# A macaron Mamba block on one core: short first and last chunks, rows loaded ahead, z's products and the gate as finer streams

## The chip, the cores and the metric

The kernel runs on one NeuronCore of one Trainium2 chip. The metric is the device time of one execution in microseconds (us), median of the runs; lower is better. The core has TensorE (PE, with its weight loads listed apart as PEld), VectorE (DVE), ScalarE (ACT), GpSimd (POOL) and SyncE (SP, which here only issues transfers). Each engine works through its own instructions in program order and waits on semaphores for the others.

## The reference, cut to what matters

x is 1 x 4096 x 1024, all in float32. Three residual steps follow one another: half a feed-forward step, a Mamba step, half a feed-forward step.

```python
def ffn(x):                      # weights rounded to -1, 0, 1 times their mean magnitude
    scale = mean(abs(weight)); w_t = clip(round(weight / (scale + EPS)), -1, 1)
    return x @ (w_t * scale).T + bias

def mamba(x):                    # D = 1024 channels, 16 states, a recurrence over 4096 tokens
    u, z = split(x @ W_in.T)
    u = silu(conv_b + sum(conv_w[:, k] * shifted(u, k) for k in range(4)))
    dt_r, B, C = split(u @ W_xproj.T)
    dt = softplus(dt_r @ W_dt.T + b_dt)
    h_t = exp(dt_t * A) * h_(t-1) + dt_t * B_t * u_t        # A = -exp(A_log)
    y_t = sum over states of h_t * C_t
    return ((y + u * Dskip) * silu(z)) @ W_out.T

x = x + 0.5 * ffn(layernorm(x)); x = x + mamba(layernorm(x)); x = x + 0.5 * ffn(layernorm(x))
```

## The kernel before

The 4096 tokens are cut into 16 chunks of T = 256 tokens, each of TT = 2 token tiles of 128. The channels lie on the partitions in 8 blocks of 128, and the recurrence is done in two halves of 4 blocks. For every chunk the kernel does, in this order of data:

- **Front** (`front`): rows are loaded (L236), normalized over channels (`stats` L390, L392, L394, L402 to L404; `normed` L409), transposed by PE (L425), split into a high and a low part (L453, L455) and multiplied with the ternary weights that stay on the chip (L497; for chunk 0, where these weights are just being made by DVE at L316 and L318, in `as_weights_come`, L528). The residual is added at L476; the bias reaches x by an accumulating transfer that POOL issues (L469). A second normalization follows, its transposes are copied to xT (L600), and PE forms the u products from W_in blocks that are streamed from memory through five shared weight buffers (L361, L629). `conv` applies the four taps (L559, L562 on ACT, L574 on DVE) and SiLU (L581).
- **Steps**: still in `front` and `rest`, PE projects u to dt_r, B and C (L641); B and C go to memory (L654) and come back spread over all partitions, one transfer for each half and state (`fetch`, L883, five bc buffers). `delta` forms dt (L710, L722). Then `rest` multiplies z's weights (L368, L677, SiLU at L696).
- **Recurrence**, for each half and state n: ACT forms the decays exp(dt A) (L913) in PSUM, POOL forms dt B u (L934) and adds what enters from the previous chunk (L941), DVE scans 2 x 2 blocks (L966, 512 columns each) and multiplies with C (L978), and PE sums over states by transposing each product into the y accumulator (`summed`, L998, 8 transposes). The skip term u * Dskip is the first of these products (L899). When a half is complete, `gate` multiplies y by silu(z) (L1015, one instruction for both token tiles).
- **Back** (`back`): the gated half is transposed back (`turned`, L752, L742), multiplied with W_out (L374, L760), added to x (L731), and the third step runs as the first did; the rows are written out (L772). The last chunk has a variant of its own (`last`), in which the first half's W_out products run before the second half is complete.

What sets the order of the work is a planner that runs while the program is built (`Streams`). Every piece of work above is a generator, a stream, that asks for an engine with an estimated duration and an earliest time; `run` always takes the request that can start first, ties by rank (the constants DECAY to FFN_C and Z), with a look-ahead `HOLD` by which an engine is kept for a better rank that is due soon. Buffers are handed round by `Buffers.take` and `put` with estimated times. The result is a fixed order on each engine and on SP's queue; on the chip each instruction then waits for what it truly needs, with everything behind it on its engine. So an instruction that is planned too early holds up its whole engine, and a transfer that waits for a buffer holds up every transfer behind it on SP's queue.

PSUM is used in full: three banks for general use, three for decays, and one double bank for y (`ys`, L998 writes it; chunk 0's first step borrows it). A chunk's y buffer is free again when its gate has read it.

Of the kernel before, what the change touches and what calls it, by code (L numbers as in the profile page):

```python
# [38 lines left out]
P = 128  # L39
T = 256  # L40
# [13 lines left out]
ISSUE, ADDED = 950, 6000  # L54
SWITCH = 1300

DECAY, ENTER, SUM, PREPARE, RECUR, GATE = 5, 1, 1, 0, 2, 2
FFN_A, NORM, U_PART, CONV, DELTA, OUT, FFN_C = 0, 0, 3, 0, 0, 2, 3

HOLD = 0, 0, 500, 100  # L60
# [3 lines left out]
class Streams:  # L64
# [32 lines left out]
    def run(self):  # L97
        hold = dict(zip(("PE", "DVE", "ACT", "POOL"), HOLD))
        while self.streams:
            todo = sorted(((self.start(s[2]), s[1], i) for i, s in enumerate(self.streams)))  # L100
# [73 lines left out]
def macaron_mamba_kernel(  # L174
# [16 lines left out]
    NC = S // T  # L191
# [10 lines left out]

    order = Streams()
# [6 lines left out]
    ys = buffers(1, [P, TT, OH], "y", pool_=psum)  # L210
    xs = buffers(6, [P, D], "x")
# [5 lines left out]
    szs = buffers(3, [P, TT, OH], "sz")  # L217
    dts = buffers(2, [P, HB, T], "dt")
    tmps = buffers(2, [P, D], "tmp")
    ups = buffers(3, [P, KER - 1 + T], "up")  # L220
# [3 lines left out]
    products = buffers(3, [P, HB, T], "p")  # L224
# [10 lines left out]
    def load_x(c, t):  # L235
        nc.sync.dma_start(x_tiles[c, t], x_in[(c * TT + t) * P : (c * TT + t + 1) * P, :])  # L236

    for t in range(TT):
        x_tiles[0, t] = xs.free.pop(0)[1]
        load_x(0, t)  # L240
# [100 lines left out]
    def streamed(load, n, ahead, rank):  # L341

        queue = []

        def fill():
            for i in range(n):
                yield lambda: 0 if len(queue) < ahead else INF
                w = yield from weights.take()
                load(i, w)
                queue.append((order.now + 5000, w))  # L350

        order.spawn(fill(), rank)
        return queue
# [26 lines left out]
    def stats(c, at, tiles=range(TT)):  # L380
# [5 lines left out]
        xn = {}  # L386
        for t in tiles:
            xn[t] = yield from tmps.take()
# [50 lines left out]
    def ffn(c, which, rank, at, tiles=range(TT)):  # L439
# [3 lines left out]
        def split(t):  # L443
# [6 lines left out]
            def cut(g, pt, at_):  # L450
# [12 lines left out]
            yield from transposed(xn, begin, cut, rank)  # L463
# [8 lines left out]
        def residual(t, cols, pf, at_):  # L472
# [4 lines left out]
            if (*key, t) != ("a", 0, 1):  # L477
                banks.put(pf, end)
# [36 lines left out]
    def as_weights_come(key, parts, residual, rank):  # L515

        for t in range(TT):
            yield from when("parts", key, t)
        y = yield from ys.take()
        groups = {(1, h): y[:, h, :] for h in range(2)}  # L520
        for h in range(2):
            groups[0, h] = yield from banks.take()
# [14 lines left out]
        for t in range(TT):  # L537
            los.put(parts[t][0], end)
            his.put(parts[t][1], end)
        for h in range(2):  # L540
            end = yield from when("ffn", key, 1, h * OH)
        ys.put(y, end)

    u, sz, dt, xd, bc_dram, over = {}, {}, {}, {}, {}, {}


    def hand_over(c, blk, up, at):
        end = yield pool(140, at)
        nc.gpsimd.tensor_copy(halo[:, blk, :], up[:, T:])
        ready["halo", c, blk] = end  # L550

    def conv(c, blk, pp, at):
        half, b = divmod(blk, HB)
        up = yield from ups.take()
        ub, rows_ = u[c, half][:, b, :], pp[:, blk % 2, :]
# [3 lines left out]
        nc.scalar.copy(up[:, KER - 1 :], rows_)  # L559
# [11 lines left out]
        for k in range(KER - 1):  # L571
            end = yield dve(405, end + (REACH if k == 0 else 115), True)
# [6 lines left out]
        if len(done) == HB:  # L579
            end = yield act(D, end + REACH, "silu")  # L580
            nc.scalar.activation(flat(u[c, half]), flat(u[c, half]), AF.Silu)  # L581
            ready["u", c, half] = end + REACH

    def front():
        for c in range(NC):
            yield FFN_A
            at = [3500, 5000]
            for t in range(TT if c else 0):
                x_tiles[c, t] = yield from xs.take()
                load_x(c, t)  # L590
                at[t] = order.now + 5000
            ends = yield from ffn(c, "a", FFN_A, at)
            yield NORM
            queue = streamed(u_weights, NB, 2, U_PART)
            ln, rows_, at = yield from stats(c, ends)
# [12 lines left out]
            for t in range(TT):  # L608
# [3 lines left out]
            for t in range(TT):  # L612
# [5 lines left out]
            for pair in range(NB // 2):  # L618
                if 2 * pair % HB == 0:
                    u[c, 2 * pair // HB] = yield from us.take()  # L620
                pp = yield from banks.take()
                pp = pp.rearrange("p (j t) -> p j t", t=T)
                for j in range(2):
                    w = yield from arrived(queue)
                    wt = w.rearrange("p (k m) -> p k m", m=P)
                    for k in range(NB):
                        if k % 4 == 0:
                            end = yield pe(8 * T * FULL)
                        nc.tensor.matmul(  # L629
                            pp[:, j, :], wt[:, k, :], xT[:, k, :], start=(k == 0), stop=(k == NB - 1)  # L630
# [3 lines left out]
            yield DELTA  # L634
            px = yield from banks.take()
            for half in range(2):
                at = yield from when("u", c, half)
                end = yield pe(2 * HB * T * FULL)
                for b in range(HB):
                    k = half * HB + b  # L640
                    nc.tensor.matmul(  # L641
                        px[:NXD, :T], wx[:, k, :], u[c, half][:, b, :], start=(k == 0), stop=(k == NB - 1)
                    )
            xd[c] = yield from xds.take()
            end = yield act(T, end + REACH)
            nc.scalar.copy(xd[c][RANK:NXD, 1, :], px[RANK:NXD, :T])
            for j in range(2):
                end = yield act(T)
                nc.scalar.copy(xd[c][j * RANK : (j + 1) * RANK, 0, :], px[:RANK, :T])
            banks.put(px, end)  # L650
            bc_dram[c] = dram.tile([NST, 2, T], F32, tag="bc", name=f"bcd_{c}")
            for j in range(2):
                part_ = slice(RANK + j * NST, RANK + (j + 1) * NST)
                nc.sync.dma_start(bc_dram[c][:, j, :], xd[c][part_, 1, :])  # L654
            ready["bc", c] = end + 2500
            yield from delta(c, 0, end + REACH)
            order.spawn(rest(c, xT), DELTA)
# [441 lines left out]
```

## Time and profile before

| | |
|---|---|
| median of 3 runs | 2726.5 us (2725.86 to 2727.03) |
| the profiled execution | 2725.84 us, its span 2724.1 us |
| busy PE / DVE / ACT / POOL | 2568.1 / 2288.3 / 2001.4 / 1815.6 us |
| first recurrence scan (DVE L966) starts | 104.2 us |
| last scan starts, last gate starts | 2668.2 us, 2675.8 us |
| moved by DMA | 410.8 MB, mean 151 GB/s |

The span is the time from the first to the last instruction on the core. Busy time is the union of an engine's instructions; PE's instructions are pipelined, so that eight listed at 1.04 us together start every 0.109 us. An idle time is put down to the instruction that ended it. Columns of the stretches of time further on: stretch, its length, busy time of the five rows with the number of instructions, the granted TensorE clock (1.00 is full), the share of time for which the DMA engines moved data, and GB/s.

### The profile page before, as it was taken

Reading aid. Unit: us, or ns where it says so; the run is one execution under the profiler, and the core shown is the slowest. Engines: PE = TensorE matmul, PEld = TensorE weight load, DVE = VectorE, ACT = ScalarE, POOL = GpSimd, SP = SyncE. Lnnn points to the kernel's source line nnn. Section 1 sums busy time; section 2 is a strip of 40 time slices with the busy share of each in tenths; the row PEclk is TensorE's granted clock in tenths of the full one; section 3 lists DMA queues with packets and bytes.
Section 4 is the critical chain, followed back from the end, with each engine's and each line's share of the span. In section 5 each row is a group of like instructions: output and inputs, shape, how many; then the busy total and the mean of one; then the engine's idle time right before and its main releaser. Section 6 shows DMA issues by size and latency. Waiting matters only on the chain. (4 is left out here: it accounts for less than half of the span.)

```text
span 2724.1 us, 41050 instructions
## 1 busy us (share of the span) xinstructions
PE 2568.1 (94%) x14082; PEld 2199.6 (81%) x14082; DVE 2288.3 (84%) x2404; ACT 2001.4 (73%) x4202; POOL 1815.6 (67%) x1657
## 2 busy tenths in 40 slices
PE   5797989999999999999999999999999999999988
PEld 4686878888788787888878788887888878788866
DVE  4498898978899798888879799898889879788883
ACT  3678677787877778777787877778787777877662
POOL 0367767766677585767757577686767857577761
PEclk9897999999999999999999999999999999999999
DMA  4443536455454545546554454655545554554533
GB/s 158 146 130 103 168 106 216 132 166 149 134 173 140 179 151 153 155 129 184 166 162 144 140 167 132 182 162 155 153 140 167 159 172 146 150 157 133 182 85 109
DMA packets 218553, 410.82 MB, mean 151 GB/s; under 512 B 19172, under 2 KB 85860, under 8 KB 218344
## 3 DMA queue, kind: packets, MB, share of 16 engines
q1 hardware_dynamic: 209128, 374.65, 43.3%
q0 software_dynamic: 9216, 33.56, 6.8%
q8 instruction: 110, 1.80, 0.3%
q14 instruction: 99, 0.81, 0.1%
HBM read 390.82 MB, written 17.31 MB: 150 GB/s over the span
## 5 line engine op out<-in xcount | busy, mean ns | idle before, releaser
L934 POOL TENSOR_TENSOR h<-u,bc 128x1024 f32<-128x1024 f32 x512 | 1223.2, 2389 | 421.7 <-ACT da L913 171.1
L966 DVE TENSOR_TENSOR_SCAN h<-da,h 128x512 f32<-128x512 f32 x1024 | 1207.7, 1206 | 125.6 <-ACT da L913 99.7
L913 ACT ACTIVATE da<-dt,pr 128x255 f32<-128x255 f32 x2048 | 938.6, 473 | 61.9 <-DVE h L966 32.9
L978 DVE TENSOR_TENSOR p<-h,bc 128x1024 f32<-128x1024 f32 x512 | 658.7, 1286 | 6.6 <-PE y L998 6.4
L998 PE MATMUL y<-ident,p 128*128 128x128 f32 x4352 | 572.5, 278 | 79.5 <-DVE p L978 61.1
L998 PEld LDWEIGHTS y<-ident,p 128*128 128x128 f32 x4352 | 503.9, 143 | 151.5 <-DVE p L978 95.4
L629 PE MATMUL bank<-xT,weight 128*128 128x256 f32 x2048 | 474.7, 382 | 11.4 <-ACT u L562 8.6
L677 PE MATMUL bank<-weight,xT 128*128 128x256 f32 x2048 | 474.7, 380 | 9.2 <-DMA weight<-in_w_in 9.2
L760 PE MATMUL bank<-weight,u 128*128 128x256 f32 x2016 | 467.3, 381 | 2.2 <-DMA weight<-in_w_out 1.9
L629 PEld LDWEIGHTS bank<-xT,weight 128*128 128x128 f32 x2048 | 378.6, 190 | 69.9 <-ACT u L562 21.3
L677 PEld LDWEIGHTS bank<-weight,xT 128*128 128x128 f32 x2048 | 380.2, 191 | 56.7 <-ACT da L913 9.9
L760 PEld LDWEIGHTS bank<-weight,u 128*128 128x128 f32 x2016 | 370.9, 191 | 47.2 <-DMA weight<-in_w_out 2.1
L949 ACT COPY state<-h 128x4 f32<-128x4 f32 x512 | 99.2, 194 | 292.5 <-DVE h L966 287.5
L941 POOL TENSOR_TENSOR h<-h,over 128x4 f32<-128x4 f32 x512 | 262.5, 513 | 25.2
L497 PE MATMUL bank<-wf,lo 128*128 128x512 f32 x976 | 252.3, 400 | 3.7 <-DVE lo L455 2.4
L574 DVE SCALAR_TENSOR_TENSOR u<-up,pr,u 128x256 f32<-128x256 f32 x384 | 206.4, 570 | 55.2 <-ACT u L562 42.6
L497 PE MATMUL bank<-wf,hi 128*128 128x512 f32 x976 | 245.8, 394 | 0.0
L497 PEld LDWEIGHTS bank<-wf,lo 128*128 128x128 f32 x976 | 177.7, 188 | 48.4 <-issue 4.0
L497 PEld LDWEIGHTS bank<-wf,hi 128*128 128x128 f32 x976 | 181.7, 188 | 43.0 <-issue 4.3
L865 POOL TENSOR_TENSOR over<-pr,dt 128x64 f32<-128x64 f32 x32 | 24.9, 778 | 211.3 <-ACT dt L722 211.3
L476 DVE SCALAR_TENSOR_TENSOR x<-bank,hscl,x 128x512 f32<-128x512 f32 x124 | 91.2, 737 | 71.9 <-PE bank L497 71.8
L425 PE MATMUL bank<-ident,tmp 128*128 128x128 f32 x756 | 115.9, 285 | 27.1 <-ACT tmp L409 23.4
(98 smaller groups left out, 2125.0 us busy)
## 6 DMA issues: line engine op xcount, KB each, us to landing
bc<-bcd SPq DMA_DIRECT2D x512, 256.0 KB, 3.7
weight<-in_w_out SPq DMA_DIRECT2D x128, 512.0 KB, 5.1
weight<-in_w_in SPq DMA_DIRECT2D x128, 512.0 KB, 3.7
weight<-in_w_in SPq DMA_DIRECT2D x256, 256.0 KB, 4.2
x<-hbias POOLq DMA_DIRECT2D x64, 512.0 KB, 7.9
x<-in_x SPq DMA_DIRECT2D x32, 512.0 KB, 7.3
out<-x SPq DMA_DIRECT2D x30, 512.0 KB, 4.9
weight<-in_w_ffn SPq DMA_DIRECT2D x5, 512.0 KB, 7.4
```

The costliest lines, as they stand in the source:

```text
L425: nc.tensor.matmul(pt[:, j * P : (j + 1) * P], xn[:, k * P : (k + 1) * P], ident, start=(j == 0), stop=(j == 3), is_transpose=True, skip_g ...
L497: nc.tensor.matmul(pf, x[:, k, :], wf[:, k, cols], start=(x is lo and k == 0), stop=(x is hi and k == NB - 1),)
L574: nc.vector.scalar_tensor_tensor(ub, up[:, k : k + T], tap, ub, ALU.mult, ALU.add)
L629: nc.tensor.matmul(pp[:, j, :], wt[:, k, :], xT[:, k, :], start=(k == 0), stop=(k == NB - 1))
L677: nc.tensor.matmul(pp[:, t, :], xT[:, k, t * P : (t + 1) * P], wt[:, :, i, :], start=(k == 0 and t == 0), stop=(k == NB - 1), skip_group_c ...
L760: nc.tensor.matmul(po[:, t, :], yT[:, b, t * P : (t + 1) * P], wt[:, b, :], start=(half == 0 and t == 0 and b == 0), stop=(half == 1 and b ...
L913: nc.scalar.activation(da[:, i, 1:], dt[c, half][:, b, 1:], AF.Exp, scale=a_neg[:, half * HB + b, n : n + 1],)
L934: nc.gpsimd.tensor_tensor(h, u[c, half], bc[:, 0:1, :].to_broadcast([P, HB, T]), ALU.mult)
L941: nc.gpsimd.tensor_tensor(h[:, :, 0], h[:, :, 0], over[c, half][:, :, n], ALU.add)
L966: nc.vector.tensor_tensor_scan(rows_, flat(da), rows_, 0.0, ALU.mult, ALU.add)
L978: nc.vector.tensor_tensor(p, h, bc[:, 1:2, :].to_broadcast([P, HB, T]), ALU.mult)
L998: nc.tensor.matmul(y[:, t, b * P : (b + 1) * P], p[:, b, t * P : (t + 1) * P], ident, start=(n < 0 and b == 0), stop=(n == NST - 1 and b = ...
```

## The change

The sequence is cut into 17 chunks: 128 tokens, 15 times 256, 128 tokens. Work tiles keep their shapes, and `cut` gives a view of the part that a short chunk uses. Further:

- `rows_ahead` is a stream of its own that loads the rows of later chunks as soon as one of the x buffers (7 for 6) is free; a buffer counts as free as soon as its output transfer is issued, where before 6 us were added.
- z's products (`gates`) and the projection with dt (`steps`) are two streams that start together when the u products have been issued; before, z's followed the projection.
- y is two single-bank buffers, one for each token tile; each tile is gated by itself when its last state has been summed, and transposed back tile by tile. Chunk 0's first step needs no y bank any more.
- Buffers: products 4 for 3, ups 4 for 3, z's sz 2 for 3; W_in's u blocks are streamed 3 ahead for 2, W_out's 2 ahead for 3.
- The planner gets other ranks, look-aheads and margins (`LATE_P`, `LATE_E`, 6,500 ns for a weight block), and a penalty `TABLE` for a request that would change ACT's function table.

```diff
-ISSUE, ADDED = 950, 6000
+ISSUE, ADDED = 950, 12000
-DECAY, ENTER, SUM, PREPARE, RECUR, GATE = 5, 1, 1, 0, 2, 2
-FFN_A, NORM, U_PART, CONV, DELTA, OUT, FFN_C = 0, 0, 3, 0, 0, 2, 3
-HOLD = 0, 0, 500, 100
+LATE_P, LATE_E = 300, 700
+AHEAD = 3
+DECAY, ENTER, SUM, PREPARE, RECUR, GATE = 5, 4, 1, 0, 5, 1
+FFN_A, NORM, U_PART, CONV, DELTA, OUT, FFN_C = 0, 4, 3, 0, 0, 2, 3
+TABLE = 300
+HOLD = 250, 0, 0, 0
...
-    NC = S // T
+    sizes = [P] + [T] * ((S - 2 * P) // T) + [P]
+    starts = [sum(sizes[:c]) for c in range(len(sizes))]
+    NC = len(sizes)
...
+    def cut(tile_, c, n):
+        t = sizes[c]
+        return flat(tile_)[:, : n * t].rearrange("p (b t) -> p b t", t=t)
...
-    ys = buffers(1, [P, TT, OH], "y", pool_=psum)
-    xs = buffers(6, [P, D], "x")
+    ys = buffers(TT, [P, OH], "y", pool_=psum)
+    xs = buffers(7, [P, D], "x")
-    szs = buffers(3, [P, TT, OH], "sz")
+    szs = buffers(2, [P, TT, OH], "sz")
-    products = buffers(3, [P, HB, T], "p")
+    products = buffers(4, [P, HB, T], "p")
...
+    def rows_ahead():
+        for c in range(1, NC):
+            for t in tiles_of(c):
+                x_tiles[c, t] = yield from xs.take()
+                load_x(c, t)
+                ready["x", c, t] = order.now + 5000
...
-            queue = streamed(u_weights, NB, 2, U_PART)
+            queue = streamed(u_weights, NB, 3, U_PART)
...
+            order.spawn(gates(c, xT), Z[0])
+            order.spawn(steps(c), DELTA)
...
-                xs.put(x_tiles.pop((c, t)), order.now + 6000)
+                xs.put(x_tiles.pop((c, t)), order.now + 0)
...
-            end = yield pe(D * TURN)
-            for t in range(TT):
+            for t in tiles_of(c):
+                if first:
+                    y[t] = yield from ys.take()
+                end = yield pe(OH * TURN)
...
+                if n + 1 == NST:
+                    order.spawn(gate(c, half, t, y[t], end + REACH), GATE)
...
-    def gate(c, half, y, at):
+    def gate(c, half, t, y, at):
         yield from when("z", c, half)
-        z = sz[c, half]
-        end = yield dve(1170, at)
-        nc.vector.tensor_tensor(flat(z), flat(y), flat(z), ALU.mult)
+        z = sz[c, half][:, t, :]
+        end = yield dve(650, at)
+        nc.vector.tensor_tensor(z, y, z, ALU.mult)
         ys.put(y, end + REACH)
-        ready["gate", c, half] = end + REACH
+        ready["gate", c, half, t] = end + REACH
...
+        (AHEAD, rows_ahead()),
```

## The prediction, made before the changed kernel was run

> **What bounds the kernel now.** I read the page's busy times first, then stretches of time, then who waits for whom on PE, then the timeline at the two ends.
>
> ```profile
> PE 2568.1 (94%) x14082; PEld 2199.6 (81%) x14082; DVE 2288.3 (84%) x2404; ACT 2001.4 (73%) x4202; POOL 1815.6 (67%) x1657
> ```
>
> PE leads, but 94% is a mean over unlike stages. The stretches separate them (columns as described with the profile above):
>
> ```profile
> 37.00:54.00 17.00, 7.04 (x32) 6.00 (x31) 3.23 (x7) 8.53 (x13) 1.69 (x6) 0.76 0.00 1
> 96.00:112.00 16.00, 6.75 (x21) 4.59 (x22) 5.09 (x5) 11.61 (x24) 9.14 (x8) 0.50 0.65 215
> 112.00:209.00 97.00, 94.59 (x524) 82.17 (x523) 85.78 (x90) 75.17 (x160) 67.07 (x69) 0.99 0.47 139
> 209.00:248.00 39.00, 22.13 (x108) 18.33 (x107) 32.44 (x31) 32.14 (x65) 29.12 (x24) 0.65 0.33 91
> 500.00:1000.00 500.00, 486.23 (x2720) 418.64 (x2719) 433.87 (x454) 383.53 (x807) 344.63 (x316) 1.00 0.52 155
> 2612.00:2625.00 13.00, 6.97 (x46) 6.34 (x47) 6.03 (x6) 11.35 (x19) 7.64 (x9) 0.79 0.12 40
> 2646.00:2672.00 26.00, 16.31 (x73) 13.75 (x73) 24.66 (x23) 11.30 (x29) 15.37 (x10) 0.67 0.53 173
> ```
>
> In the long middle PE is 97.2% busy at full clock: it is the bound there, and DVE (87%) is not. At the start and the end there are holes, and in each the granted clock falls too (0.50 to 0.79), so what PE still does in them is stretched. In the middle the remaining idle time has few owners (microseconds, times, longest, from 500 to 2500 us):
>
> ```profile
> PE y L998 <- DVE p L978: 21.6, 31, 1.3
> PE y L998 <- DVE sz L1015: 14.5, 11, 1.3
> PE bank L752 <- DVE x L476: 9.3, 11, 0.8
> ```
>
> The gate waits at L1015 recur once per chunk: 11 stand between 819.1 and 2445.8 us, so a chunk takes 162.67 us, and 16 take 2602.7. The span is 2724.1, so 121.4 us are the price of filling and draining. The timeline of the hole at 230 us shows what it is:
>
> ```profile
> 230.25 1.97 PE L998 MATMUL y<-ident,p 128*128 128x128 f32 x8 [6.70 <-DVE p L978]
> 233.81 1.97 PE L998 MATMUL y<-ident,p 128*128 128x128 f32 x8 [1.60 <-DVE p L978]
> ```
>
> PE has nothing left but one sum per state, waits for DVE's product each time, and at the low clock takes 1.97 us for eight transposes that take 1.04 elsewhere. The page's chain of waits agrees for the other end: its last 55 us are PE lines L760 and L497.
>
> **The change, part by part.** *The yardstick.* Fifteen full chunks and two halves are again 16 chunk equivalents, so 2602.7 us stay as long as the middle's pace stays. To be priced are the fill, the drain, the pace, and what an extra chunk adds to PE. PE's rates at full clock, from the timeline: 0.229 us for a matmul of 512 columns (L497), 0.216 for 256 (L629: eight in 1.73), 0.109 for a transpose of 128 (L998: eight in 0.87).
>
> *An extra chunk on PE.* u and the projection stream half the columns per weight block in a short chunk; the other products count by token tile and don't change. A pass of 128 columns is not in the trace; from below it is half of 0.216, from above the 0.143 us of one weight load (L998's PEld). 320 such passes in the two short chunks: 0 to +11 us. I take 0, since transposes, which have the same shape, start every 0.109.
>
> *The fill.* "Lost" is the length less PE's work at full rate. Before: until the first step's last matmul at 40.9, 16 transposes and 64 matmuls are 16.4 us of work, lost 24.5; the second normalization to 50.8, lost 9.9; transposes and u to 88.5, lost 7.4; projection and dt to 112, lost 14.9; 112 to 209, 3.4; the hole to 248, 16.9 idle and 0.35 of 22.1 by the clock, 24.6. Sum 84.7.
>
> After, the order on the engines is known, the times are not. DVE makes the ternary weights until 37.2 as before, but with 32 matmuls in place of 64 PE ends 1.2 us later, at 38.4: work 8.2, lost 30.2, which is 5.7 *more* than before. One tile's residual (two L476, 1.5 us) and one tile's normalization (5.3 us, as the tail's single tile takes from L390 to L425) reach 45.2: lost 6.8. u is 128 passes of 0.109, or 13.9 us; the supply is slower, since three buffers turn over in landing 3.7 + use 1.75 + issue 0.6 = 6.0 us, 2.0 a block, 16 for eight, and I take 17: ends 63, lost 2.7. Projection, dt, the first bc and the first scan took 15.7 us and have fixed parts (table loads 1.28, the transfer out and in 1.5 + 3.7); I take 13.5, so the first scan moves from 104.2 to about 77. PE need not stand still there: with z's stream apart, the order has three z blocks (5.2 us) and chunk 1's transposes and first step (16.4 us) next, whose rows are there; lost 4. Then chunk 0's recurrence: per state two scans of 1.165/2 and a product of 1.2/2 us, each with about 0.065 of fixed cost on top, 1.96 us, times 32 is 63 us, with chunk 1's conv and splits on DVE about 80. PE's work for this time is 14.8 (sums) + 8.6 (z) + 14.7 + 1.75 + 27.7 + 1.7 = 69; before it was about 107 against 118 of recurrence alone with as much added. A hole of 12 stays. Sum 56, so **-29**; with the old hole whole -16, with none -41.
>
> *Rows ahead.* Six row loads (3 MB) now stand on SP's queue before hbias, W_out and W_in. Until 40 us, 9.7 MB moved before (300 and 184 GB/s in the two 20 us stretches), now 12.2; at 300 GB/s that is 41 us, so it fits under the ternary stage and the normalization with 4 us to spare. Nothing taken; if not hidden, up to +4 of the 13 above.
>
> *The drain.* Before, 2600 to 2724 loses 24.7 idle and 8.9 by clock, 33.6 in all: the hole at 2612, the lone sums at 2646 to 2672, and the last step. After, the last recurrence is 63 us instead of 113 and has chunk 15's W_out and third step (27.6 + 14.7) beside 14.8 of sums; in the order only six sums are left after the last of it, each about 1.9 us with 0.9 of work, so -7 there, and about -3 at the first hole. Against it, the single last tile has nothing beside its normalization, where before the first tile's ran under W_out: 7.2 us from L731 to L455 against 3.4 exposed, +4. **-6**, from -15 to +5.
>
> *The pace.* Gate by tile: a sum for tile 0 of the next half needs only tile 0's gate, issued while tile 1 is summed. That removes the 14.5 us row but for one wait in six, -12 in 2000 us; DVE pays 32 gates more at a fixed 0.127 (402 ns for 256 columns at L731, 677 for 512 at L455), 4 us, under its 13% of slack. The later planned readiness of products and the fourth product buffer act on the 21.6, the shorter bank cycles on the 9.3; nothing shows how far, from all of it to none. I take a quarter, -8. That is -20 per 2000 us, 1.6 per chunk, **-24** over 15; all waits gone is 4.1 a chunk, -62. In the other direction I allow +1 a chunk, +15: two sz buffers for three, and SP below. Table loads on ACT fall from 181 to 175; ACT is idle 27%, nothing.
>
> A rule of the Trainium skill speaks against the short chunks: "Perfetto Trace Analysis", section "Optimizing Scalar/DVE Operations", puts about 60 ns of fixed cost on each DVE instruction and advises larger ones. By it the 162 added DVE instructions would be 10 us; the rows' 0.13 us make 21. The sum is the same by both, as DVE's slack covers either, and only in the 80 us after the first scan does it lengthen DVE's path, which the 1.96 us holds already.
>
> *Sum.* 2724.1 - 29 - 6 - 24 + 0 = 2665, and 1.7 us around the span gives 2667; the median runs 0.7 above the profiled execution: **2668**.
>
> **The rivals.**
>
> 1. *Only the ends gain.* The margins merely move the waits on PE and the pace stays 162.7: 2726.5 - 35 = 2692. For it: the 31 waits on p are each under 1.3 us, jitter of a plan rather than a structure. Against: the gate wait is structural and comes once per chunk.
> 2. *All of it.* The waits in the middle nearly vanish and the start has no hole: -41 - 6 - 50, 2630. Against: PE's order still waits for some engine in every row.
> 3. *SP's queue (slower).* In the new order the load into an x buffer stands right behind the output from the same buffer, and behind it the other output, two W_out blocks and bc loads. Before, this wait (SP L236 for the output) was 2.3 us in six times; an output lands after 4.9. Fifteen times 4.9 is 74 us; if all reach PE and the pace gains nothing, 2726.5 - 35 + 74 = 2765. It decides from 2.3 us a chunk. Against: four bc transfers go out just before, a buffer's turn is 5 x 3.53 = 17.7 us, of which landing and use take about 12, so some 6 us are slack.
> 4. *The start doesn't move.* u starves on W_in, or the six row loads delay the weights, and the first scan stays past 95 us: about 2710 with some pace gained.
>
> **How the numbers follow.** Forecast 0.50 (its own range 2652 to 2684), rival 1 0.22, rival 2 0.10, rival 3 0.10, rival 4 0.08. About 0.2%, 5 us, is what this kernel's measurement can tell. Slower holds rival 3 (0.10), no change a third of rival 4 (0.03), faster the rest, 0.87. The range takes in the forecast, rival 1, rival 4 to its middle and the near half of rival 2: 2636 to 2708.
>
> **What would show it.** First scan near 77 us (rows above 95: rival 4). No stretch of 39 us at clock 0.65 after it. A chunk period of 161 us from gate to gate and the row PE y <- DVE gate under 3 us in 2000 (162.7: rival 1). SP's row-load wait for the output: expected about 5 us a chunk, with no PE wait for W_out or DVE wait for bc behind it; if these appear, rival 3. The prediction is wrong if the middle's PE share falls below 97%, or if the last tile's chain is longer than the sums it replaces.

## The result, and the profile after

The changed kernel takes **2698.03 us** (median of 4 runs, 2693.4 to 2698.7) against 2726.24 us for the kernel before, measured beside it: a ratio of 0.9893, 95% interval 0.988 to 0.9905. It is 28 us faster; 58 were forecast. The time lies outside the forecast's own range (2652 to 2684) and nearest to rival 1 (2692); only the wide range, which takes the rivals in, holds it. The profiled span is 2696.9 us.

Busy times of the changed kernel, as listed on its page:

```profile
PE 2567.8 (95%) x14242; PEld 2199.8 (82%) x14242; DVE 2320.2 (86%) x2564; ACT 2017.8 (75%) x4401; POOL 1773.4 (66%) x1747
```

PE is as busy as before (2568.1), to 0.3 us: the whole gain is idle time. Stretches of the changed kernel (columns as in the table before; the bounds are its own events: end of the first step, start and end of chunk 0's u, first scan, chunk 1's first scan, and the drain):

```profile
38.40:45.40 7.00, 1.83 (x9) 1.61 (x9) 0.00 (x0) 4.11 (x6) 1.31 (x5) 0.50 0.00 0
45.40:69.70 24.30, 19.95 (x134) 18.48 (x134) 7.24 (x21) 8.97 (x23) 2.15 (x14) 0.85 0.52 156
69.70:90.50 20.80, 17.06 (x83) 14.15 (x82) 4.51 (x10) 16.02 (x32) 6.18 (x13) 0.84 0.60 162
90.50:201.70 111.20, 100.50 (x520) 82.73 (x520) 84.59 (x133) 93.33 (x243) 64.25 (x97) 0.98 0.44 131
500.00:1000.00 500.00, 485.98 (x2711) 416.86 (x2710) 450.76 (x470) 379.55 (x816) 340.49 (x323) 1.00 0.53 156
1500.00:2000.00 500.00, 492.14 (x2750) 423.76 (x2749) 441.14 (x468) 385.02 (x816) 344.20 (x323) 1.00 0.52 157
2657.00:2674.50 17.50, 16.82 (x72) 13.95 (x72) 1.97 (x4) 0.59 (x1) 0.00 (x0) 0.90 0.56 181
2674.50:2696.90 22.40, 11.92 (x41) 9.15 (x40) 3.31 (x5) 4.80 (x7) 2.15 (x5) 0.77 0.19 47
```

The 39 us at clock 0.65 behind the first recurrence are gone (0.98 up to chunk 1's first scan). The middle has two parts: from 500 to 1000 us PE is no busier than before (486.23), and only later does it reach 98.4%. The end has a stretch of 22.4 us in which PE works for half the time. PE's waits from 500 to 2500 us, and SP's row for the loads of x (waited for: us, times, longest):

```profile
PE bank L653 <- ACT u L578: 10.2, 14, 1.7
PE bank L784 <- DVE x L496: 8.8, 11, 0.8
PE bank L445 <- ACT sz L721: 5.2, 11, 1.4
PE y L1045 <- DVE p L1022: 4.7, 11, 0.5
...
PE y L1045 <- DVE sz L1062: 0.3, 1, 0.3
...
SPq L256 <- DMA out<-x: 47.4, 22, 4.6
```

The waits on products fell from 21.6 to 4.7 us, those on the gate from 14.5 to 0.3; the waits for banks that ACT reads grew (10.2 and 5.2 us; before, u's had 2.4 and sz's no row). SP waits 47.4 us for outputs in front of row loads, and no wait of PE for W_out or of DVE for bc stands behind it.

**Where the time came from.** I use the prediction's measure, "lost" = time less PE's work so far at full rate. That work is 2472.2 us in all, at the prediction's rates and 0.136 us for each of dt's matmuls, so that the span is 2472.2 plus what is lost; matmuls that run slower than the prediction's rate count as lost too. The loss is cut by PE's work done, and the period is the distance of the chunks' first scans, a mean over six chunks in the steady part. The experiments are in the same table, so that it can be read beside them (medians as each run has them, the other columns from the profiled execution; us):

| kernel | lost to 200 of work | 200 to 1000 | 1000 to 2350 | from 2350 | period | median |
|---|---|---|---|---|---|---|
| before | 90.7 | 52.4 | 71.5 | 37.2 | 162.6 | 2726.2 |
| changed | 76.0 | 52.5 | 57.9 | 38.3 | 160.7 | 2698.0 |
| pad | 70.7 | 51.4 | 56.7 | 39.4 | 160.7 | 2695.3 |
| uniform | 103.5 | 44.7 | 54.2 | 27.4 | 160.7 | 2705.0 |
| defer | 107.1 | 50.1 | 57.2 | 39.6 | 160.7 | 2727.7 |
| first2 | 109.9 | 58.5 | 55.2 | 27.5 | 160.7 | 2722.3 |
| wholegate | 79.8 | 68.1 | 145.3 | 38.4 | 169.3 | 2805.2 |
| tilegate | 91.7 | 82.4 | 103.4 | 36.4 | 166.4 | 2792.5 |
| oldconst | 114.3 | 79.2 | 88.1 | 38.9 | 162.1 | 2794.6 |
| serialz | 96.8 | 67.6 | 96.6 | 37.0 | 164.8 | 2777.3 |
| norows | 80.9 | 81.6 | 96.6 | 47.9 | 168.3 | 2782.1 |
| upback | 74.9 | 51.8 | 56.7 | 38.1 | 160.6 | 2694.9 |
| drainfill | 74.4 | 53.1 | 57.8 | 34.5 | 160.7 | 2691.2 |
| both | 74.0 | 52.0 | 56.4 | 33.9 | 160.6 | 2690.4 |

Against the kernel before, the change gains 14.7 at the start, nothing from 200 to 1000 us of work, 13.6 in the rest of the middle, and loses 1.1 in the drain: 27.2, the difference of the spans. One caution on small differences: the changed kernel and pad have the same instructions in the same order, and their first columns differ by 5.3; the changed kernel's profiled execution is the slowest of its four (2698.7), pad's the fastest of its four (2692.2).

### The profile page after: what moved, and what is told of

Read it like the earlier page. It is cut to its first block, busy times and chain, and to the rows that moved or that the text cites. A ratio compares the mean times of both kernels' runs of the same rounds, so it can differ in the third digit from the quotient of the medians.

```text
span 2696.9 us, 41854 instructions
## 1 busy us (share of the span) xinstructions
PE 2567.8 (95%) x14242; PEld 2199.8 (82%) x14242; DVE 2320.2 (86%) x2564; ACT 2017.8 (75%) x4401; POOL 1773.4 (66%) x1747
## 4 chain that ended last, share of the span: by engine, by line
PE 33%; ACT 7%; DVE 7%; issue 4%; POOL 4%; DMA 0%; POOLq 0%; DVEq 0%; SPq 0%
PE bank L516 8%; PE bank L792 6%; PE bank L653 6%; PE y L1045 5%; PE bank L706 5%; DVE h L1009 3%; DVE p L1022 3%; POOL h L977 2%; ACT da L955 2%; PE bank L671 1%; PE bank L445 1%; ACT tmp L414 1%; ACT tmp L429 1%; ACT u L578 1%; ACT dt L754 1%
## 5 line engine op out<-in xcount | busy, mean ns | idle before, releaser
L977 POOL TENSOR_TENSOR h<-u,bc 128x1024 f32<-128x1024 f32 (+1 forms) x544 | 1230.5, 2262 | 419.1 <-ACT da L955 206.6
L1009 DVE TENSOR_TENSOR_SCAN h<-da,h 128x512 f32<-128x512 f32 (+1 forms) x1088 | 1216.7, 1143 | 132.4 <-ACT da L955 68.7
L955 ACT ACTIVATE da<-dt,pr 128x255 f32<-128x255 f32 (+1 forms) x2176 | 982.5, 462 | 381.9 <-DVE h L1009 341.2
L1022 DVE TENSOR_TENSOR p<-h,bc 128x1024 f32<-128x1024 f32 (+1 forms) x544 | 695.0, 1278 | 0.1
L1045 PEld LDWEIGHTS y<-ident,p 128*128 128x128 f32 x4352 | 505.7, 142 | 83.2 <-DVE p L1022 28.8
L653 PE MATMUL bank<-xT,weight 128*128 128x256 f32 (+1 forms) x2176 | 476.6, 372 | 20.9 <-ACT u L578 17.6
L706 PE MATMUL bank<-weight,xT 128*128 128x256 f32 x2048 | 487.1, 383 | 3.8 <-ACT sz L721 1.4
L516 PE MATMUL bank<-wf,lo 128*128 128x512 f32 x1008 | 268.9, 409 | 4.4 <-DVE x L496 2.5
L516 PE MATMUL bank<-wf,hi 128*128 128x512 f32 x1008 | 259.5, 399 | 0.0
L590 DVE SCALAR_TENSOR_TENSOR u<-up,pr,u 128x256 f32<-128x256 f32 (+1 forms) x408 | 197.5, 517 | 48.8 <-POOL up L573 22.8
L516 PEld LDWEIGHTS bank<-wf,lo 128*128 128x128 f32 x1008 | 185.6, 191 | 52.3 <-DVE x L496 6.4
L516 PEld LDWEIGHTS bank<-wf,hi 128*128 128x128 f32 x1008 | 187.4, 189 | 46.6 <-issue 3.3
L445 PE MATMUL bank<-ident,tmp 128*128 128x128 f32 x760 | 115.9, 281 | 33.9 <-ACT tmp L429 22.4
L445 PEld LDWEIGHTS bank<-ident,tmp 128*128 128x128 f32 x760 | 93.5, 144 | 53.8 <-ACT tmp L429 24.3
```

Source lines behind the costliest of these rows:

```text
L445: nc.tensor.matmul(pt[:, j * P : (j + 1) * P], xn[:, k * P : (k + 1) * P], ident, start=(j == 0), stop=(j == 3), is_transpose=True, skip_g ...
L516: nc.tensor.matmul(pf, x[:, k, :], wf[:, k, cols], start=(x is lo and k == 0), stop=(x is hi and k == NB - 1),)
L590: nc.vector.scalar_tensor_tensor(ub, up[:, k : k + T], tap, ub, ALU.mult, ALU.add)
L653: nc.tensor.matmul(pp[:, j, :T], wt[:, k, :], xT[:, k, :T], start=(k == 0), stop=(k == NB - 1))
L706: nc.tensor.matmul(pp[:, t, :], xT[:, k, t * P : (t + 1) * P], wt[:, :, i, :], start=(k == 0 and t == 0), stop=(k == NB - 1), skip_group_c ...
L955: nc.scalar.activation(da[:, i, 1:], dt[c, half][:, b, 1:], AF.Exp, scale=a_neg[:, half * HB + b, n : n + 1],)
```

## The experiments

Every kernel is the changed one with the edit shown, but for tilegate, which starts from the kernel before. The kernel before ran beside each (2725.3 to 2726.5 us); ratios are to it.

### The sizes: uniform, first2, defer

**uniform** has 16 equal chunks and all the rest of the change; the only further edits are that chunk 0's first step borrows the y banks, as before, and that the clearing of decay banks for a short last chunk falls away.

```diff
-    sizes = [P] + [T] * ((S - 2 * P) // T) + [P]
+    sizes = [T] * (S // T)
```

> The changed kernel with 16 equal chunks of 256 tokens, all else kept (chunk 0's first step borrows the two y banks for its second tile). By PE's work done (0.229, 0.216 and 0.109 us an instruction) the changed kernel had lost 15 us less than the one before after 200 us of work, and nothing less in the drain. Theory 'short chunks filled': the fill's 15 come from the short first chunk; without it 2712, with about 90 us lost after 200 us of work and a hole at low clock after the first scans. Theory 'streams filled': they come from rows ahead and z's own stream; 2698 within 4, with the first scan near 100 us all the same.

Measured: 2704.99 us, ratio 0.9917 [0.9898, 0.9937]. This lies between the two theories. All of the change but its short chunks gives 21.5 of the 28 us. The short first chunk saves 27.5 us at the start (103.5 to 76.0), but from there to 2350 us of work the uniform kernel loses 11.5 us less, and in the drain 10.9 less. And the 27.5 are not the forecast's 29, which were counted from the kernel before: uniform loses 12.8 us *more* at the start than that kernel (103.5 against 90.7). Its first scan comes at 128.9 us, when much of PE's other work is done, and from then to chunk 1's first scan at 290 us PE has this row (the kernel before, from 60 to 264 us: 16.7, 7, 6.7):

```profile
PE y L1045 <- DVE p L1022: 27.3, 14, 3.9
```

So the rest of the change costs at the start, and the short chunk wins that back and 14.7 more. Its last stretches, at the same times as two of the kernel before (uniform ends 22 us earlier):

```profile
2612.00:2625.00 13.00, 13.00 (x65) 11.22 (x64) 12.10 (x12) 11.53 (x24) 9.30 (x8) 0.87 0.63 139
2646.00:2672.00 26.00, 25.76 (x140) 22.79 (x139) 8.61 (x12) 3.50 (x7) 2.80 (x3) 1.00 0.20 62
```

PE is busy throughout, at full clock in the second, where the kernel before had holes. The drain loses 27.4 for 37.2 without short chunks: the rest of the change mends it, and a short last chunk takes that back.

**first2** puts both short chunks at the start.

```diff
-    sizes = [P] + [T] * ((S - 2 * P) // T) + [P]
+    sizes = [P, P] + [T] * ((S - 2 * P) // T)
```

> The changed kernel with both short chunks at the start (sizes 128, 128, then 15 times 256), nothing else changed; it ends on a full chunk. Theory A, that the single tile at the end costs the drain about 11 us (27.4 us of lost PE time behind 2350 us with equal chunks against 38.3 with a short last one) and that the first short chunk's gain of 27 us in the fill stays: 2698 - 11 = 2687, with no hole of 5 us on PE after the last U-part sum and the last tile's normalization beside the other tile's W_out. Theory B, that the loss in the drain comes of the streams and of the gate by tile: 2698, the drain as long as before. Theory C, that a second short chunk right behind the first starves PE again (its recurrence is as short as its work for the chunk behind it): 2705 or more, with a new hole between 100 and 250 us.

Measured: 2722.34 us, ratio 0.9985 [0.9975, 0.9994]. C holds, in time and place: the start loses 34 more. Of A the drain's part holds (it loses 27.5, as uniform's), its time does not. From 160 to 240 us, the changed kernel first and then first2, which has PE 64 us busy of 80 at clock 0.83 in it:

```profile
160.00:240.00 80.00, 75.69 (x414) 63.70 (x414) 60.56 (x75) 70.92 (x162) 50.64 (x56) 1.00 0.52 156
```

```profile
160.00:240.00 80.00, 63.73 (x318) 52.56 (x317) 56.00 (x86) 60.88 (x172) 45.47 (x64) 0.83 0.42 126
```

I read it so: a short chunk leaves PE too little work to stand beside the recurrence of the chunk ahead of it, and only the first has none ahead.

**defer** holds chunk 1's first step back until chunk 0's first decays, since the first scan came 20.8 us after u's end (forecast 13.5) with ACT at work on chunk 1 in between.

```diff
             yield FFN_A
             at = [3500, 5000]
+            if c == 1:
+                yield from when("decay", 0, 0, 0, 0)
```

> The changed kernel with chunk 1's first step held back until chunk 0's first decays have been issued, so that ACT and DVE go straight from dt to the first scan. In the changed kernel the first scan stood at 90.5 us, 20.8 after u's last product, behind chunk 1's statistics, normalization and splits. Theory 'queued behind': this late scan is what the fill lost against the forecast; first scan near 82 and 4 to 8 us faster, 2692. Theory 'PE's work sets it': the first step of chunk 1 is what PE has to do in that time; the scan comes earlier and the time gets 3 to 10 us worse, 2704.

Measured: 2727.72 us, ratio 1.0004 [0.9994, 1.0014]. The first scan is at 81.5 in place of 90.5, and the kernel 30 us slower: chunk 1's first scan moves from 201.7 to 238.2. From 60 to 240 us PE has this row, which the changed kernel does not have in that time:

```profile
PE y L1047 <- DVE p L1024: 19.4, 13, 4.8
```

This is the direction of the second theory at three times the most that it allowed: a first scan 9 us earlier does not pay for chunk 1's work coming later, so how early PE has that work counts for more than the first scan, whose lateness I had taken for the loss.

### One part away, or one part alone: wholegate, tilegate, oldconst, serialz, norows

**wholegate**: y is one double bank again and one gate serves both tiles.

```diff
-    ys = buffers(TT, [P, OH], "y", pool_=psum)
+    ys = buffers(1, [P, TT, OH], "y", pool_=psum)
...
-    def gate(c, half, t, y, at):
+    def gate(c, half, y, at):
```

> The changed kernel with y as one double bank again and one gate instruction for a half, as before. Theory 'gate': the pace in the middle (160.7 us a chunk against 162.6) comes mostly from this; the wait of PE's sums for the gate comes back with some 15 us in 2000, pace 162, time +15 to +20: 2715. Theory 'margins': the later planned products and the ranks made the pace; the wait comes back with under 8 us, time +2 to +8: 2703.

Measured: 2805.2 us, ratio 1.0285 [1.0264, 1.0305], 107 us slower than the changed kernel. PE's longest rows from 500 to 2500 us:

```profile
PE bank L792 <- DMA weight<-in_w_out: 34.7, 13, 4.2
PE bank L653 <- ACT u L578: 23.6, 25, 1.7
PE bank L445 <- ACT sz L721: 12.6, 11, 1.3
```

Neither theory holds: the gate itself isn't among them. PE waits for W_out blocks that come late, of which the changed kernel has no row in that time. At 1157 and at 2000 us, for instance, SP's queue has an output, a row load that waits some 4 us, the other output and two W_out blocks, and PE then waits. From 1000 to 2500 us SP has this row, where the changed kernel has 31.1, 16, 3.4:

```profile
SPq L256 <- DMA out<-x: 60.0, 17, 4.7
```

This is what rival 3 described, brought about by another edit; other W_out blocks come late with a bc load in front of them.

**tilegate**: the kernel before with y in two banks and a gate for each tile, nothing else.

> The kernel before with one part of the change alone: y in two banks of one token tile each, a sum and a gate for each tile, 16 equal chunks, the old streams, ranks and margins. Forecast's working: the row of PE waiting for the gate (14.5 us from 500 to 2500 us) nearly goes, DVE pays 4 us a 2000 us under its slack: 2726 - 12 to -15, about 2712, period 161.8. Theory B, that the gate by tile is what lets the whole new plan hold (taking it out of the changed kernel cost 107 us): more than 20 us faster. Theory C, that the two tiles need the new streams and ranks to gain anything: 2722 to 2732, the waits on the gate replaced by waits on p or on the banks.

Measured: 2792.54 us, ratio 1.0241 [1.0226, 1.0256], 66 us *slower* than the kernel it starts from; no theory foresaw that. Rows from 500 to 2500 us:

```profile
PE y L999 <- DVE p L978: 16.4, 13, 1.6
PE bank L629 <- ACT u L562: 15.2, 19, 0.9
PE bank L425 <- ACT tmp L409: 13.6, 13, 1.2
PE bank L752 <- DVE x L476: 10.3, 11, 1.8
PE y L999 <- DVE sz L1016: 6.2, 10, 0.6
```

The gate's row does fall, from 14.5 to 6.2, and the rows on ACT for u and tmp rise from 2.4 and nothing to 28.8: the period is 3.8 us longer.

**oldconst**: the changed structure with the ranks, margins, holds and table penalty of before.

```diff
-ISSUE, ADDED = 950, 12000
+ISSUE, ADDED = 950, 6000
-LATE_P, LATE_E = 300, 700
+LATE_P, LATE_E = 0, 0
-DECAY, ENTER, SUM, PREPARE, RECUR, GATE = 5, 4, 1, 0, 5, 1
+DECAY, ENTER, SUM, PREPARE, RECUR, GATE = 5, 1, 1, 0, 2, 2
-FFN_A, NORM, U_PART, CONV, DELTA, OUT, FFN_C = 0, 4, 3, 0, 0, 2, 3
+FFN_A, NORM, U_PART, CONV, DELTA, OUT, FFN_C = 0, 0, 3, 0, 0, 2, 3
-TABLE = 300
-HOLD = 250, 0, 0, 0
+TABLE = 0
+HOLD = 0, 0, 500, 100
```

> The changed kernel with the ranks, margins, holds and table penalty of the kernel before (all the structure of the change, none of its numbers). Theory A, that the new numbers make the steady pace (row y<-p 21.6 to 4.7 us): 15 to 25 us slower than the changed kernel, 2713 to 2723, with the waits on p back at 20 us from 500 to 2500 us. Theory B, that the structure makes it (third set of product buffers, gate by tile): within 5 us of 2698. Theory C, that the old ranks do not fit the new streams (GATE at 2 behind the steps, NORM at 0): over 2740 with waits on W_out or the gate.

Measured: 2794.57 us, ratio 1.0248 [1.0232, 1.0263]. C by its bound, though PE has no row for W_out or the gate from 500 to 2500 us; A in one row: y<-p is back at 28.4 us. The period is only 1.4 us longer than the changed kernel's; two thirds of the loss lie at the start (38 more) and in the next 800 us of work (27 more).

**serialz**: z's products behind the projection again.

```diff
-            order.spawn(gates(c, xT), Z[0])
-            order.spawn(steps(c), DELTA)
+            order.spawn(steps(c, xT), DELTA)
...
         xds.put(xd[c], order.now + 2000)
+        order.spawn(gates(c, xT), Z[0])
```

> The changed kernel with z's products again behind the last step of the projection of the same chunk, as in the kernel before, in place of a stream of their own; rows, gate by tile, sizes and numbers stay. Theory A, that PE has other work to fill in the start (chunk 1's transposes and first step) and that z is only moved: 2698 to 2704, the lost time up to 200 us within 4 us of the changed kernel's 76. Theory B, that z beside the first recurrence is what fills the start: 8 to 15 us slower, lost time up to 200 us 85 or more, with PE waiting for gates' z in the first chunk.

Measured: 2777.25 us, ratio 1.0185 [1.0168, 1.0202]. B in its place (96.8 lost at the start) but not in its wait nor its size: from 80 to 260 us PE waits for products (16.6 us), not for z, and 79 us are lost, 39 of them between 1000 and 2350 us of work, with a period of 164.8.

**norows**: rows loaded at the front of their own chunk.

```diff
-                at[t] = yield from when("x", c, t)
+                x_tiles[c, t] = yield from xs.take()
+                load_x(c, t)
+                at[t] = order.now + 5000
...
-        (AHEAD, rows_ahead()),
```

> The changed kernel without the stream for the rows: each chunk's rows are loaded where the chunk's front begins, as in the kernel before; all else stays. Theory A (rival 3 turned round), that the row loads' waits on SP's queue (47 us of waiting for the output from the same buffer) cost something that is hidden in the pace: 5 to 15 us faster. Theory B, that they cost nothing and gain a little at the start, where chunk 1's rows are there early: 2698 to 2706, the loss up to 200 us of PE work up by 4 to 8. Theory C, that any other order of the loads upsets the plan, as four of the six single changes did: 2725 or more, with waits of PE in the middle that the changed kernel does not have.

Measured: 2782.11 us, ratio 1.0203 [1.0188, 1.0218]: C. PE now waits 4.8 us for W_out from 1000 to 2300 us, and 13.9 for banks that ACT reads (L578; the changed kernel has 4.7 up to 2500 us). From 1000 to 1500 us, the changed kernel and then norows:

```profile
1000.00:1500.00 500.00, 491.50 (x2728) 421.76 (x2728) 441.12 (x469) 380.66 (x811) 338.93 (x318) 1.00 0.53 158
```

```profile
1000.00:1500.00 500.00, 478.59 (x2638) 408.81 (x2636) 435.85 (x451) 370.44 (x789) 326.66 (x311) 0.99 0.51 151
```

All five end 51 to 79 us slower than the *kernel before*. Four parts that each cost 79 to 107 us when taken away cannot sum to a gain of 28: as I read it, what is measured is mostly the order that the planner builds anew after the edit. Where the order stays the same instruction for instruction (pad, upback), the time stays within some 3 us. And the steady period is the same, 160.6 to 160.7, in all kernels with the change's structure and numbers, whatever the sizes and the start. Which part of the change makes it isn't shown. What each part would be worth with numbers chosen for the rest wasn't tried and stays open.

### FFN's matmuls: pad, upback

The 512-column matmuls start every 229.4 ns in the kernel before and every 233.6 ns in the changed one, over 2048 of them some 8 us. **pad** moves wf by 32 bytes to a multiple of 64:

```diff
-    thr = const.tile([P, 2], F32, name="thr")
+    thr = const.tile([P, 16], F32, name="thr")
```

> The changed kernel with 32 bytes more in one small tile, so that the ternary weights wf, allocated behind it, start at a multiple of 64 bytes again, as in the kernel before (189120); in the changed kernel they start at 194272, which is 32 past one. No instruction moves. Theory 'address': the third step's and first step's matmuls (L516) start every 233.4 ns in place of 229.4 because of the address; back to 229.4, about 2047 of them, -8 us: 2690. Theory 'neighbours': they are slower for what runs beside them (transfers, other engines); 233.4 stays, and the time stays within 2 us of 2698.

Measured: 2695.27 us, ratio 0.9885 [0.9868, 0.9901], matmuls every 232.5 ns: not the multiple of 64. **upback** puts the fourth up buffer behind wf:

```diff
-    ups = buffers(4, [P, KER - 1 + T], "up")
+    ups = buffers(3, [P, KER - 1 + T], "up")
...
     wf = const.tile([P, NB, D], F32R, name="wf")
+    ups.free.append((0.0, const.tile([P, KER - 1 + T], F32, name="up3")))
```

> The changed kernel with the same instructions in the same order on every engine; only the fourth up buffer stands behind wf in SBUF in place of before it, so that wf and what stands between the ups and wf begin 1056 bytes lower, at the positions that they have in the kernel before plus 4096 bytes. Theory A, that the FFN's matmuls of 512 columns take 233.6 ns in place of 229.4 because of where wf lies (2048 of them, 4.2 ns each): FFN start to start 229.4, about 8.6 us faster than the changed kernel, 2689. Theory B, that the pace of these matmuls comes from what runs beside them (DVE, ACT, DMA) or from the order: 233.6 as before, 2698.

Measured: 2694.91 us, ratio 0.9888 [0.9873, 0.9903], matmuls every 229.5 ns: A for the pace. Both kernels have the same instructions in the same order on PE, DVE, ACT and POOL. That it was another chip is not it: drainfill, with wf where the changed kernel has it, ran on the same chip as upback and keeps 233.6, and **both** (below), with upback's places, has 229.4 on another. The page's rows of L516 in the changed kernel, and of the same line, L517, in upback:

```profile
L516 PE MATMUL bank<-wf,lo 128*128 128x512 f32 x1008 | 268.9, 409 | 4.4 <-DVE x L496 2.5
L516 PE MATMUL bank<-wf,hi 128*128 128x512 f32 x1008 | 259.5, 399 | 0.0
```

```profile
L517 PE MATMUL bank<-wf,lo 128*128 128x512 f32 x1008 | 265.6, 406 | 4.9 <-DVE x L497 2.4
L517 PE MATMUL bank<-wf,hi 128*128 128x512 f32 x1008 | 255.6, 396 | 0.0
```

Not for the time: it fell by 3, not by 8.6, and even 3 is within the scatter (the intervals of the two ratios overlap). In the steady part FFN gives 0.43 us a chunk, while idle time grows by 0.20 and the sums' time by 0.12; the period falls by 0.13. So here most of what the faster matmuls gave was lost again elsewhere on the same engine.

### The drain: drainfill, and both together

The changed kernel's end on PE, in order of time (start, length, what, idle before and releaser):

```profile
2672.62 1.89 PE L792 MATMUL da<-weight,u 128*128 128x256 f32 x8
2680.28 1.97 PE L445 MATMUL da<-ident,tmp 128*128 128x128 f32 x8 [5.77 <-ACT tmp L429]
2682.80 3.78 PE L516 MATMUL bank<-wf,lo 128*128 128x512 f32 x8 [0.55 <-DVE lo L475]
2686.38 2.63 PE L516 MATMUL bank<-wf,hi 128*128 128x512 f32 x8
```

Between the last W_out product and the single tile's transposes PE has nothing for 5.77 us, and the first eight FFN matmuls behind it take 3.78 us in place of 2.03. **drainfill** keeps other work for the hole:

```diff
-            ends = yield from ffn(c, "c", FFN_C, [end, end], tiles_of(c))
...
+            if c + 2 < NC:
+                yield from third(c, end)
+            else:
+                order.spawn(third(c, end), FFN_C)
         yield from last(NC - 1)
...
             begin = yield from when("parts", key, t)
+            if key == ("c", NC - 2) and t == 1:
+                yield from when("closed")
...
             order.spawn(finished(c, t), FFN_C)
+        ready["closed",] = end
```

> The changed kernel with one change in the drain: chunk 15's third step is a stream of its own beside the last chunk's output projection, and its second tile's matmuls (7.5 us) are held until PE has issued the last W_out product, so that they stand in the hole of 5.8 us that the last tile's normalization leaves (last eight W_out products at 2672.6, next PE work at 2680.3, then eight FFN matmuls in 3.78 us in place of 1.87). Theory A, that the drain lost what the forecast promised to this hole and to the low clock behind it: W_out's first half moves ahead of the last sums, the hole goes, PE stays at full clock; 8 to 12 us faster, 2686 to 2690, lost time behind 2350 us of PE work 26 to 30 in place of 38.3. Theory B, that the last recurrence (ends at 2655.8) and the chain from it set the end whatever PE does beside it: within 4 us of 2698.

Measured: 2691.17 us, ratio 0.9871 [0.9855, 0.9888]. The same place in it:

```profile
2668.93 1.89 PE L794 MATMUL da<-weight,u 128*128 128x256 f32 x8
2670.47 2.23 PE L518 MATMUL da<-wf,lo 128*128 128x512 f32 x8
...
2678.14 1.03 PE L445 MATMUL bank<-ident,tmp 128*128 128x128 f32 x8
2680.13 2.13 PE L518 MATMUL bank<-wf,lo 128*128 128x512 f32 x8 [0.96 <-DVE lo L475]
```

The hole is filled and the clock holds. The time lies between the two theories. From the last W_out product on, 6.0 us are lost in place of 14.2, as A has it; but in front of it 4.4 more are lost (28.5 for 24.1), so only 3.8 are gained in the drain (38.3 to 34.5): the last recurrence now ends at 2659.2 in place of 2655.8, with sums behind W_out groups of 16. B has its part. Another 1.6 us of the 4.9 between the two spans stand at the start (74.4 for 76.0), where both kernels are the same; that is scatter, as with pad.

**both** has the edits of upback and of drainfill.

> The changed kernel with the drain's held-back tile and the fourth up buffer behind wf together. If the two gains are of different places (3 us measured for the position, 7 for the drain) they add: 2688, FFN start to start 229.5, lost time behind 2350 us of PE work near 34.5 as with the held-back tile alone. If the drain's gain was scatter between runs (the same program's start differed by 4 to 6 us in the lost time at 80 us), it falls back to 2692 to 2695.

Measured: 2690.39 us (2688.2 to 2692.1), ratio 0.9872 [0.9856, 0.9889]: between the two expectations. It beats the kernel before clearly. All its runs lie below all of the changed kernel's, but they were taken at another time, and the intervals of the two ratios overlap at 0.988 to 0.9889.

## Why the prediction was half right

**The fill (-29; measured -14.7).** The first two steps came as worked out: the first step ended at 37.4 (38.4), the normalization at 45.4 (45.2), 36.2 lost there (37.0). The step that failed is "u is 128 passes of 0.109 [...] the supply is slower [...] I take 17". It took 24.3, and the supply of W_in was not the limit; PE has no wait for a transfer in it:

```profile
60.40 1.16 PE L653 MATMUL bank<-xT,weight 128*128 128x128 f32 x8 [0.76 <-ACT u L578]
62.80 1.35 PE L1045 MATMUL y<-ident,p 128*128 128x128 f32 x4 [1.24 <-ACT p L933]
68.67 1.16 PE L653 MATMUL bank<-xT,weight 128*128 128x128 f32 x8 [0.77 <-ACT u L578]
```

PE was idle for 4.35 us, in waits of some 0.7 for the banks that ACT's taps read and one of 1.24 for a skip product. Busy time was 19.95 for 14.3 of work, in part since the granted clock was 0.59 up to 50 us, behind a wait of 6.10, and 0.79 from 60 to 65, where PE worked 3.36 us of 5. In the kernel before, a u of twice the columns had a clock of 1.00 from 60 us on. The Trainium skill, "TensorE: Matmul & The Clock Gate", section "HAM oscillation — how this bites in real kernels", tells of a kernel in which some 2 us of work stand between waits of 3 to 5 us, and the gate slows PE at each. The waits inside u are shorter, 0.72 to 1.24 us, so these rows show the slow clock but not that rule.

Of the terms behind it, up to the first scan 7.9 were lost for 4, and 17.1 for the hole of 12: chunk 0's recurrence took 105 us for 80. DVE's own work in it was nearly as forecast (82.7 us for "63 us, with chunk 1's conv and splits on DVE about 80"); what that term left out is that DVE waits, 16.0 us for ACT and 8.8 for POOL. Its longest rows from 90.5 to 195.2 us:

```profile
DVE h L1009 <- ACT da L955: 8.6, 7, 2.2
DVE h L1009 <- POOL h L984: 6.2, 4, 4.3
```

Sum 71.2 at chunk 1's first scan, forecast 56. The forecast's sum for the kernel before is low as well: counted as in the table, that kernel has lost 89.6 at 248 us, not 84.7.

**The pace (-24; measured -13.5 over the whole middle).** Its size came out where it holds: 1.85 us a chunk for 1.6, the gate's row 0.3 us, 161 from gate to gate, and PE at 98.4%. In part that was luck. From 500 to 2500 us PE's waits fell by 17.2 us for the forecast's 20, but the waits on products and on x's banks fell by 17.4, twice the "quarter" that was taken, and "ACT is idle 27%, nothing" failed: the waits for banks that ACT reads rose from 2.6 to 18.4. The step that failed in the sum is the factor "1.6 per chunk [...] over 15". Up to 1000 us of work nothing is gained. The chunks' first scans stand 154.4, 145.2, 153.4, 158.4 and 162.6 us apart before the steady 161, and DVE is busy 450.8 us of the 500 up to 1000 us (433.9 before): PE, ahead of the chunks' work by 53 us at chunk 1's first scan, has some 3.5 left at 975.8. In uniform that stretch loses 7.8 less. That it is DVE that the lead is lost to is read from its busy time and not shown by a run. PE's own waits between these two scans are 14.7 us on DVE and 12.0 on banks that ACT reads, so ACT may have a share. Defer, which starts as late as uniform, loses 50.1 there, so part of it may belong to the short chunk's order.

**The drain (-6; measured +1.1).** Two terms were mis-sized. For "the single last tile has nothing beside its normalization [...] +4" it is +6.0: from the last W_out product on, 14.2 us are lost for 8.2 before, in the hole of 5.77 and at the slow clock behind it, and drainfill, which fills the hole, brings that to 6.0. For the lone sums and the first hole, -7 and -3, it is -4.9: PE's waits for products from 2600 us on fell from 15.0 to 4.3 us, but a wait of 4.61 for the normalization of chunk 15's rows stands at 2627.81. So the prediction's own sign of being wrong, a last tile's chain longer than the sums it replaces, came true by this count.

**The rest.** The extra chunk's 128-column passes for u start every 0.112 us in the median and 0.115 in the mean in the last chunk, at full clock, and those of the projection every 0.109: some 1.5 us over u's 256, within 0 to 11. The rows ahead were hidden: PE has no wait for a transfer up to 202 us. The Trainium skill's section that the prediction cites ("Perfetto Trace Analysis", "Optimizing Scalar/DVE Operations") gives its 60 ns for a DVE instruction on SBUF, and about 125 ns on PSUM. Both rows behind the forecast's 0.13 us read PSUM, so page and rows agree.

**The rivals.** "Only the ends gain" gave the nearest time, 2692, for a wrong reason: the ends gave 13.6 of their 35, and the pace as much again. SP's queue had the wait that it named (47.4 us, some 4 a chunk) and nothing behind it; wholegate shows what it looks like when W_out does come late. "The start doesn't move" needed a first scan past 95; it was at 90.5, and defer shows that this mark says little.

## What to carry to other kernels

Time won at the start need not last (against uniform, 27.5 us won at the start were 16.0 by 2350 us of PE's work): follow the loss by stage to the end before adding gains, and multiply a gain per chunk only by the chunks that are steady. A last unit made short needs work kept back to stand beside its chain, and here that gave back only 3.8 us of 10.9, since the work in front of it was upset. Where a planner builds the order, taking out one part measures the new order as much as the part; test parts with the order held, or choose the numbers anew for each.

## What the runs showed of the hardware

The pace of the 512-column matmuls depends on where things lie in SBUF: the same order (the changed kernel, pad, upback) runs at 233.6, 232.5 or 229.5 ns a matmul with wf at 194272, 194304 or 193216 bytes (in the kernel before 189120, 229.4). The last two differ by 4096 bytes; a multiple of 64 is not what matters. Tiles between the ups and wf moved along, so which operand it is stays open.

In the changed kernel's drain, after 5.77 us without work, PE worked for 7 us or so, with one break of 0.55, before it reached its full rate: the eight matmuls from 2686.38 still took 2.63 us, and the next eight 2.03.
